# A graph layer on one core: stores of u four slots behind a block's end, reads of u five slots ahead, and the last group's blocks in one line

## The chip, the cores and the metric

The kernel runs on one core of a Trainium2 chip. The metric is the device time of one execution in microseconds, as the median of several runs. A profiled execution gives a page of the busy times and a trace of every instruction. The engines are named TensorE (PE), VectorE (DVE), ScalarE (ACT), GpSimd (POOL) and SyncE (SP, which only issues transfers here).

## The reference

The layer is a relational graph convolution with a highway gate, on 1250 nodes of 1024 features and 20000 edges of 8 types, all in float32:

```python
h = jnp.maximum(_layernorm(x, axis=-1), 0.0)
# with x := h inside the layer
msgs = x[src]
out = x @ root + bias
for r in range(8):
    mask = (edge_type == r).astype(x.dtype)
    sums = jax.ops.segment_sum(msgs * mask[:, None], dst, num_segments=n)
    cnt = jax.ops.segment_sum(mask, dst, num_segments=n)
    out = out + (sums / jnp.maximum(cnt, 1.0)[:, None]) @ weight[r]
u = out
z = jnp.concatenate([u, x], axis=1) @ w_gate + b_gate
result = x_in + jnp.tanh(u) * z + x * (1.0 - z)
```

The kernel uses that a weighted sum of rows can be taken after the product: it computes y = h @ weight[r] for all nodes first, and then adds to each target node the rows of y that its edges name, each times one over the count.

## The kernel before, in words

**Products.** The 1250 nodes are ten blocks of 128 (the last has 98 rows). There are eleven matrices, numbered s: eight relations (s = 0 to 7), root (s = 8), and the two halves of w_gate (s = 9 for h, the last one for u). One call of `step(s, i)` makes the product of two blocks, i and i+5, with matrix s, for i = 0 to 4, so that 50 steps come before the gate. `product` uses Strassen's scheme with seven half-sized products (L283). For s > 0 the first four steps are taken in pairs, and one of the seven is itself split a second time (class `Second`, L210); the pieces are slotted between the others by the table `fill`, whose keys say behind which of the seven they come. For a pair, the first row of the even step is complete only in the odd step: it is held in `waiting`, finished by L237, L238 (for i = 0) or L241 (for i = 2), and then stored by `put` (L380, on SP's queue). For s = 8 and 9, `put` adds a bias on DVE first (L375).

**Row buffers.** Each step takes two row buffers, t[0] and t[1], from a pool of four. ScalarE writes the first product into t[0] (L312), the second into t[1] (L316), the third into t[0] again (L320); DVE adds the others from PSUM (L297, L305). A buffer is free again when its store has landed.

**Edges.** The relations form three groups (0 to 2, 3 to 5, 6 and 7), numbered g. For each group the edges of a node are sorted into slots: the nodes are ordered by their number of edges, and for each block d of the ordered nodes, slot k holds the k-th edge of each. `K[g][d]` is the number of slots of a block: 20, 10, 8, 7, 7, 6, 5, 5, 4, 3 in the first two groups, and 16, 7, 6, 5, 4, 4, 3, 3, 2, 2 in the last. `add_slot` issues one gather on POOL (L1008, rows of y into one of four buffers `got`) and one DVE instruction that adds them, weighted, to the block's sum u (L1016; L1014 for the first of all). The sum of a block starts from what the group before stored: `new_u` takes one of four buffers `u` and reads it back by an indirect DMA on POOL (L463 in a helper). When a block is done, its u is scattered to `u_dram` by an indirect DMA on POOL (L469). In the last group, blocks 4 to 9 go to `last_dram` on SP's queue (`to_last`, L1213) and are read again in the gate; blocks 0 to 3 are held in their buffers and get the row of h @ root added (`add_hr`, L1220).

**Order.** The program is issued in the order written, and each engine keeps its own order. `edges` is a generator that yields once per slot. `spread` advances it evenly between the pieces of the products (seven calls `between(j)` per step), so a gather, an add or a store of the edges stands in the queues of POOL, DVE and SP at a fixed place among the instructions of the products. The first group's edges run beside s = 4 and 5, the second's beside s = 6 and 7, the last's beside s = 8 and 9. In `edges` before, the store of a block and the read of the block after next both come behind slot 1 of the next block; the last group runs two such generators one after the other, blocks 4 to 9 and then 0 to 3 (`held`).

Of the kernel before, what the change touches and what calls it, by code (L numbers as in the profile page):

```python
# [19 lines left out]
def tile_rgcn_highway(  # L20
# [43 lines left out]
    ND = -(-N // P)  # L64
    NP = ND // 2
# [3 lines left out]
    R0 = (0, 3, 6, R)  # L69
# [8 lines left out]
    FAR = 1 << 20  # L78
    CG = 4
    GOT = 4  # L80
    LATE = 4

    A11, A12, A22, S1, S2, S3, S4 = range(7)
# [272 lines left out]
    def paired(s, i):  # L356

        return s > 0 and i < NP // 2 * 2
# [2 lines left out]

    def step(s, i, between=lambda j: None):

        t = [rows.tile([P, D], F32, name="row") for _ in range(2)]
        two = paired(s, i)
        if two and i % 2 == 0:
            waiting[i] = Second(fac[s], i), t[0]

        def put(i, part, t):
            d = i + part * NP  # L370
            n = nrows(d)
            at = slice(d * P, d * P + n)
            if s >= ROOT:
                to = (hr_dram, z_dram)[s - ROOT][at, :]
                nc.vector.tensor_add(t, t, bias_bc)  # L375
            else:
                g = max(k for k in range(G) if R0[k] <= s)
                o = (s - R0[g]) * N + d * P
                to = y[g][o:o + n, :]
            nc.sync.dma_start(to, t[:n])  # L380

        def beside(j):
            new = fac[s + 1]
            if i == 0 and j == 0 and s > 0:
                fac[s].make_t4()
            if two and i == 0:
                sums(j)
            if two and (i, j) == (1, 6):
                Second(fac[s], 2).left()
            if (s, i, j) == (0, 0, 3) or (s > 0 and (i, j) == (3, 0)):  # L390
                new.load_first()
            if (s, i, j) == (0, 0, 3) or (s > 0 and (i, j) == (3, 2)):
                new.load_next()
            if i == NP - 1:
                if j == 0:
                    new.load_b22()
                elif j == 1:
                    new.make_t1()
                elif j == 3:
                    new.load_b21()  # L400
                    new.make_t2()
                elif j == 4:
                    new.make_t3()
            between(j)

        def sums(j):


            e = waiting[0][0]
            for k in range(4) if s > R0[1] and j == 0 else (j,) if s <= R0[1] and j < 4 else ():  # L410
                e.right(k)
            if j == (0 if s > R0[1] else 4):
                e.left()

        fill = {}
        if two:
            e, to = waiting[i - i % 2]
            if i == 0:
                fill = dict(sixth=lambda: (e.second(), e.second_to_first(to)))
            elif i == 1:  # L420
                fill = dict(first=lambda: e.first(),
                            fifth=lambda: (e.sixth(), True),
                            sixth=lambda: (e.seventh(), e.to_first(to), 0)[-1],
                            seventh=lambda: (e.fourth(), e.to_second(t[0]), 0)[-1],
                            third=lambda: (e.fourth_to_second(t[0]), put(i - 1, 0, to), 0)[-1])
            elif i == 2:
                fill = dict(sixth=lambda: e.first(),
                            seventh=lambda: e.sixth(),
                            third=lambda: (e.seventh(), e.to_first(to), 0)[-1],
                            fourth=lambda: (e.fourth(), True))  # L430
            else:
                fill = dict(first=lambda: (e.to_second(t[0]), e.fourth_to_second(t[0]), 0)[-1],
                            sixth=lambda: (e.second(), True),
                            seventh=lambda: (e.second_to_first(to), put(i - 1, 0, to), 0)[-1])
        product(h_op[i], fac[s], t, between=beside, whole=not two, fill=fill)
        for part in range(2):
            if part or not two or i % 2:
                put(i, part, t[part])
# [543 lines left out]

    with ExitStack() as edges_part:
        gpool = edges_part.enter_context(tc.tile_pool(name="gpool", bufs=GOT))
        upool = edges_part.enter_context(tc.tile_pool(name="upool", bufs=4))
        bias_bc = edges_part.enter_context(tc.tile_pool(name="bpool", bufs=1)).tile(
            [P, D], F32, name="bias_bc")
        nc.sync.dma_start(bias_bc, bias[None, :].to_broadcast([P, D]))
# [16 lines left out]
        def add_slot(u, g, d, k, at, w, first=False):  # L1005
            n = nrows(d)
            t = got()
            nc.gpsimd.indirect_dma_start(  # L1008
                out=t[:n], out_offset=None, in_=y[g][:, :],
                in_offset=bass.IndirectOffsetOnAxis(ap=at[:n, d, k:k + 1], axis=0),  # L1010
                bounds_check=y[g].shape[0] - 1, oob_is_err=False)
            w = w[:n, d, k:k + 1]
            if first:
                nc.vector.tensor_scalar(u[:n], t[:n], w, None, op0=OP.mult)  # L1014
            else:
                nc.vector.scalar_tensor_tensor(u[:n], t[:n], w, u[:n], op0=OP.mult, op1=OP.add)  # L1016
# [3 lines left out]
        def new_u(d, of=None, g=0):  # L1020

            n = nrows(d)
            u = upool.tile([P, D], F32, name="u")
            if of is not None:
                rows_of(u[:n], of[:, :], node[:n, g, d:d + 1])
            return u

        def edges(g, blocks, to, late=0):


            of = u_dram[g - 1] if g else None
            ahead = new_u(blocks[0], of, g)
            behind = []
            for _ in range(late):
                yield

            def leave():
                while behind:
                    to(*behind.pop())

            for d in blocks:
                u = ahead
                last = K[g][d] - 1
                for k in range(last + 1):
                    add_slot(u, g, d, k, idx[:, g], w_of[:, g], first=g == 0 and k == 0)
                    if k == min(1, last):
                        leave()
                        if d != blocks[-1]:
                            ahead = new_u(d + 1, of, g)
                    yield  # L1050
                behind.append((d, u))
            leave()
            yield

        def u_back(g):
            def to(d, u):
                n = nrows(d)
                to_rows(u_dram[g][:, :], u[:n], node[:n, g, d:d + 1], f"u{g}")

            return to  # L1060
# [42 lines left out]
        def beside(e, total, s, i, last):  # L1103


            between = spread(e, total, 7 * ((last - s) * NP + NP - i))
            while s <= last:
                step(s, i, between)
                s, i = next(steps, (NM, 0))
            return s, i  # L1110
# [13 lines left out]
        def with_others(e):  # L1124

            others = other_groups()
            for k, _ in enumerate(e):
                yield
                if k % 2:
                    next(others, None)  # L1130
            for _ in others:
                pass

        weights(0)
        s, i = beside(with_others(edges(0, range(ND), u_back(0))), sum(K[0]) + 1, s, i,
                      R0[2] - 1)
        def with_passes(e):
            passes = passes_needed()
# [4 lines left out]
        for g in range(1, G - 1):  # L1143
            e = edges(g, range(ND), u_back(g), LATE)
            e = with_passes(e) if g == G - 2 else e
            next(e)
            s, i = beside(e, sum(K[g]) + LATE, s, i, R0[g + 2] - 1)


        passes = nc.values_load(n_pass[0:1, 0:1], min_val=0, max_val=E // MORE,  # L1150
# [64 lines left out]
        def add_hr(d, u):  # L1215
            n = nrows(d)
            t = got()
            rows_of(t[:n], hr_dram[:, :], node[:n, LG, d:d + 1])
            us[d] = u
            return lambda: nc.vector.tensor_add(u[:n], u[:n], t[:n])  # L1220

        def in_turn(*es):
            for e in es:
                yield from e

        def place_of(what, i, part):

            o = ("z", "d").index(what)
# [55 lines left out]
                while adds:  # L1284
                    adds.pop(0)()

        def held():

            new, old = [], []
            for _ in edges(LG, range(HELD), lambda d, u: new.append(add_hr(d, u))):  # L1290
                yield
                for add in old:
                    add()
                old, new[:] = new[:], []
            for add in old + new:
                add()

        late = edges(LG, range(HELD, ND), to_last, LATE + 1)
        next(late)
        between = spread(in_turn(late, held()), sum(K[LG]) + 2 + LATE, 7 * ((NM - 2 - s) * NP + NP - i))  # L1300
        while s < NM - 1:
            def beside_h(j):
                between(j)
# [69 lines left out]
```

## Time and profile before

| | |
|---|---|
| median of 3 runs | 1382.97 us (1379.1 to 1385.62) |
| profiled execution | 1378.6 us, of which the profile's span is 1376.8 us |
| busy: PE, DVE, POOL, ACT | 1353.1, 928.6, 632.6, 365.3 us |
| L1008, gathers of y on POOL | 202 issues, 252.0 us busy, 6.3 us from issue to landing |
| L1016, adds of edges on DVE | 192, 245.5 us, 1281 ns each |
| L469, stores of u on POOL | 20 issues, 26.4 us |
| u read back from u_dram | 20 issues, 7.3 us from issue to landing |

An engine's busy time counts its own instructions, not the time of the transfers that it issues. A row of the profile names the line, the engine, the operation and what it writes and reads (out<-in), and often, in brackets or behind a bar, the idle time of the engine before it and what ended that. "us to landing" is the time from the issue of a transfer to the semaphore that tells of its end. The granted clock is the share of full speed at which TensorE was allowed to run.

### The profile page before, as it was taken

The page shows a single profiled execution, that of the slowest core. Times are in us where ns is not written, and L with a number is a line of the kernel's source. Part 1 is how long each engine was busy: PE and PEld are TensorE (multiplying, and loading weights), DVE is VectorE, ACT ScalarE, POOL GpSimd, SP SyncE. Part 2 cuts the span into 40 slices and gives each one's busy share as a digit, 9 for nine tenths or more (in the row PEclk, how much of TensorE's full clock was granted, in tenths as well). Part 3 has the DMA queues.
Part 4 walks back from the last instruction along what each step waited for, and adds up shares of the span by engine and source line. Part 5 has one row for each costly group of instructions (what it writes and reads, how often), then busy time and mean ns, then how long its engine had stood idle before and what let it go on. Part 6 is the DMA issues. An engine that isn't in the chain of part 4 may idle for free.

```text
span 1376.8 us, 12702 instructions
## 1 busy us (share of the span) xinstructions
PE 1353.1 (98%) x3786; PEld 656.9 (48%) x3786; DVE 928.6 (67%) x1842; ACT 365.3 (27%) x793; POOL 632.6 (46%) x567
## 2 busy tenths in 40 slices
PE   7999999999999999999999999999999999999997
PEld 4544455445545544544554454455445445544443
DVE  6956977897768826547455854854566674567985
ACT  3335666566621111111111111111111111121220
POOL 0003655665561634667674533455535433335641
PEclk9999999999999999999999999999999999999999
DMA  8764655854653285359879736877959752687861
GB/s 303 286 203 98 130 118 137 204 97 134 138 140 104 65 229 114 118 198 263 227 243 330 246 112 220 309 253 241 338 166 325 271 189 94 216 280 241 286 201 58
DMA packets 110011, 272.78 MB, mean 198 GB/s; under 512 B 25906, under 2 KB 27936, under 8 KB 109808
## 3 DMA queue, kind: packets, MB, share of 16 engines
q0 software_dynamic: 48864, 128.60, 30.0%
q1 hardware_dynamic: 45232, 111.86, 26.4%
q10 hardware_dynamic: 15840, 31.46, 7.1%
q8 instruction: 30, 0.49, 0.1%
q14 instruction: 45, 0.37, 0.1%
HBM read 214.20 MB, written 80.65 MB: 214 GB/s over the span
## 4 chain that ended last, share of the span: by engine, by line
PE 70%; issue 8%; DVE 6%; DMA 6%; POOL 3%; ACT 1%; POOLq 0%; DVEq 0%; ACTq 0%
PE ps L283 62%; PE ps L210 7%; DMA got<-y,idx 4%; POOL got L1008 2%; DMA u_dram<-u,node 1%; DMA w<-in_L_gnn_weight_dram 1%; PE ps_n L755 0%; DVE seen L760 0%; DVE u L1016 0%; DVE junk L820 0%; DMA y<-row 0%; DMA u<-last_dram 0%; DMA got<-h_dram,node 0%; DVE row L1321 0%; DVE h_op L1257 0%
## 5 line engine op out<-in xcount | busy, mean ns | idle before, releaser
L283 PE MATMUL ps<-w,h_op 128*128 128x512 f32 x2800 | 1232.1, 594 | 2.9 <-ACT row L316 2.7
L283 PEld LDWEIGHTS ps<-w,h_op 128*128 128x128 f32 x2800 | 525.9, 191 | 606.5 <-issue 590.9
L1008 POOL DMA_INDIRECT got<-y,idx x202 | 252.0, 1248 | 268.7 <-DVE u L1016 177.5
L1016 DVE SCALAR_TENSOR_TENSOR u<-got,w_of,u 128x1024 f32<-128x1024 f32 (+1 forms) x192 | 245.5, 1281 | 161.7 <-DMA got<-y,idx 152.6
L834 POOL DMA_INDIRECT table<-row_col,at_i x157 | 176.4, 1123 | 150.4 <-DVE at_i L830 71.2
L305 DVE TENSOR_TENSOR row<-row,part 128x512 f32<-128x512 f32 x55 | 37.8, 688 | 94.4 <-ACT part L304 94.4
L338 ACT COPY row<-ps 128x512 f32<-128x512 f32 x50 | 29.3, 585 | 237.0 <-PE ps L283 231.3
L304 ACT COPY part<-ps 128x512 f32<-128x512 f32 x55 | 32.1, 584 | 181.4 <-PE ps L283 181.4
L312 ACT COPY row<-ps 128x512 f32<-128x512 f32 x55 | 32.2, 585 | 168.2 <-PE ps L283 165.3
L297 DVE TENSOR_TENSOR row<-row,ps 128x512 f32<-128x512 f32 x55 | 37.5, 683 | 57.9 <-PE ps L283 48.7
L210 PE MATMUL ps<-w,w 128*128 128x256 f32 x288 | 71.5, 381 | 0.0
L316 ACT COPY row<-ps 128x512 f32<-128x512 f32 x55 | 32.2, 585 | 141.6 <-PE ps L283 124.6
L320 ACT COPY row<-ps 128x512 f32<-128x512 f32 x55 | 32.2, 585 | 139.8 <-PE ps L283 139.6
L210 PEld LDWEIGHTS ps<-w,w 128*128 128x128 f32 x288 | 54.1, 190 | 19.0 <-issue 13.4
L469 POOL DMA_INDIRECT u_dram<-u,node x20 | 26.4, 1318 | 73.2 <-DVE u L1016 67.1
L820 DVE SCALAR_TENSOR_TENSOR junk<-k_bc,key_col,before 128x128 f32<-128x128 int32 x157 | 54.9, 350 | 4.2
L500 POOL DMA_INDIRECT node_dram<-ids,pos_i x30 | 38.6, 1285 | 39.3 <-issue 38.7
L210 PE MATMUL ps<-w,h_op 128*128 128x256 f32 x216 | 56.3, 383 | 0.0
L760 DVE TENSOR_TENSOR seen<-seen,ps_n 128x110 f32<-128x110 f32 x157 | 42.1, 268 | 16.8 <-PE ps_n L755 12.7
L210 PEld LDWEIGHTS ps<-w,h_op 128*128 128x128 f32 x216 | 40.1, 190 | 23.0 <-issue 19.9
L737 ACT ACTIVATE is_lo<-io,less_lo 128x128 bf16<-128x128 f32 x157 | 50.1, 390 | 0.9 <-DVE row L305 0.9
L888 DVE SCALAR_TENSOR_TENSOR junk<-v_bc,val,one 128x1280 bf16<-128x1280 f32 x30 | 46.5, 1550 | 4.1 <-DMA v_bc<-val_dram 3.3
(182 smaller groups left out, 948.6 us busy)
## 6 DMA issues: line engine op xcount, KB each, us to landing
y<-row SPq DMA_DIRECT2D x72, 512.0 KB, 6.5
w<-in_L_gnn_weight_dram ACTq DMA_DIRECT2D x21, 1024.0 KB, 9.4
w<-in_L_gnn_weight_dram SPq DMA_DIRECT2D x11, 1024.0 KB, 9.3
k_bc<-keys_dram SPq DMA_DIRECT2D x39, 256.0 KB, 4.0
l_bc<-los_dram SPq DMA_DIRECT2D x39, 256.0 KB, 5.9
w<-in_L_gnn_w_gate_dram ACTq DMA_DIRECT2D x6, 1024.0 KB
h_dram<-h_op SPq DMA_DIRECT2D x9, 512.0 KB, 6.9
hr_dram<-row SPq DMA_DIRECT2D x9, 512.0 KB, 6.1
```

The costliest lines, as they stand in the source:

```text
L210: nc.tensor.matmul(p, a[:, k, :], b[:, k, :], start=(fresh and k == 0), stop=(k == 1), skip_group_check=True)
L283: nc.tensor.matmul(b[:, at], aop[:, i, k, :], w.of[i][:, k, at], start=(fresh and k == 0), stop=(k == KQ - 1), skip_group_check=True)
L297: nc.vector.tensor_add(c12, c12, c)
L305: nc.vector.tensor_add(c22, c22, d)
L500: ins = nc.gpsimd.indirect_dma_start(out=node_dram[g][:, :], out_offset=bass.IndirectOffsetOnAxis(ap=pos_i[:, g, d:d + 1], axis=0), in_=id ...
L737: nc.scalar.activation(is_lo[:, i, :], io, AF.Abs, bias=less_lo[:, c0 + i:c0 + i + 1])
L760: nc.vector.tensor_add(seen[j][:, i, :], was, p[:, i, :])
L820: nc.vector.scalar_tensor_tensor(junk, o["k_bc"][:, i, :], key_col[:, c:c + 1], before, op0=OP.is_equal, op1=OP.mult, accum_out=rank[:, c: ...
L834: ins = nc.gpsimd.indirect_dma_start(out=table[:, :], out_offset=bass.IndirectOffsetOnAxis(ap=at_i[:n, i:i + 1], axis=0), in_=row_col[:n, ...
L888: nc.vector.scalar_tensor_tensor(junk, v_bc[:, g, :], val[:, c:c + 1], one.to_broadcast([P, KEYS]), op0=OP.is_gt, op1=OP.mult, accum_out=p ...
L1008: nc.gpsimd.indirect_dma_start(out=t[:n], out_offset=None, in_=y[g][:, :], in_offset=bass.IndirectOffsetOnAxis(ap=at[:n, d, k:k + 1], axis=0),
L1016: nc.vector.scalar_tensor_tensor(u[:n], t[:n], w, u[:n], op0=OP.mult, op1=OP.add)
```

## The change

The generator `edges` is written anew around one counter t, the slot. For each block it works out where its slots start (`starts`), when its u leaves (`leaves`: four slots, GOT, after the last slot) and when its u is read (`reads`: five slots before the first, but not before the store that frees its buffer has been issued). What a store returns, the addition of the row of hr, is carried out three slots later. The generator yields six times more after its last slot than before it did, most of which fall to the last call of a group. The last group is one line of blocks, 4 to 9 and then 0 to 3, instead of two generators; `in_turn` and `held` go. Each group's number of calls grows by one.

In `step`, the two row buffers are exchanged for i = 2, and the held row of i = 0 is put one piece earlier (behind the "seventh" instead of the "third").

```diff
+    UB = 4
...
+        two = paired(s, i)
         t = [rows.tile([P, D], F32, name="row") for _ in range(2)]
-        two = paired(s, i)
+        if two and i == 2:
+            t.reverse()
...
-                            seventh=lambda: (e.fourth(), e.to_second(t[0]), 0)[-1],
-                            third=lambda: (e.fourth_to_second(t[0]), put(i - 1, 0, to), 0)[-1])
+                            seventh=lambda: (e.fourth(), e.to_second(t[0]), put(i - 1, 0, to),
+                                             0)[-1],
+                            third=lambda: (e.fourth_to_second(t[0]), 0)[-1])
...
         def edges(g, blocks, to, late=0):
             of = u_dram[g - 1] if g else None
-            ahead = new_u(blocks[0], of, g)
-            behind = []
-            for _ in range(late):
+            nb = len(blocks)
+            starts = [late + sum(K[g][d] for d in blocks[:b]) for b in range(nb + 1)]
+            leaves = [starts[b + 1] - 1 + GOT for b in range(nb)]
+            reads = [max(-1, starts[b] - 5, leaves[b - UB] if b >= UB else -1) for b in range(nb)]
+            u, then = {}, {}
+            for t in range(-1, leaves[-1] + 4):
+                for b, d in enumerate(blocks):
+                    if starts[b] <= t < starts[b + 1]:
+                        k = t - starts[b]
+                        add_slot(u[d], g, d, k, idx[:, g], w_of[:, g], first=g == 0 and k == 0)
+                for b, d in enumerate(blocks):
+                    if t == leaves[b]:
+                        then[t + 3] = to(d, u[d])
+                if then.get(t):
+                    then[t]()
+                for b, d in enumerate(blocks):
+                    if t == reads[b]:
+                        u[d] = new_u(d, of, g)
                 yield
-            def leave():
-                while behind:
-                    to(*behind.pop())
-            for d in blocks:
-                u = ahead
-                last = K[g][d] - 1
-                for k in range(last + 1):
-                    add_slot(u, g, d, k, idx[:, g], w_of[:, g], first=g == 0 and k == 0)
-                    if k == min(1, last):
-                        leave()
-                        if d != blocks[-1]:
-                            ahead = new_u(d + 1, of, g)
-                    yield
-                behind.append((d, u))
-            leave()
-            yield
...
-        late = edges(LG, range(HELD, ND), to_last, LATE + 1)
-        next(late)
-        between = spread(in_turn(late, held()), sum(K[LG]) + 2 + LATE, 7 * ((NM - 2 - s) * NP + NP - i))
+        blocks = [*range(HELD, ND), *range(HELD)]
+        last = edges(LG, blocks, lambda d, u: (add_hr if d < HELD else to_last)(d, u), LATE)
+        next(last)
+        between = spread(last, sum(K[LG]) + 2 + LATE, 7 * ((NM - 2 - s) * NP + NP - i))
```

More of the change, by code (lines that the diff above doesn't have):

```diff
@@ L984, in tile_rgcn_highway @@
         gpool = edges_part.enter_context(tc.tile_pool(name="gpool", bufs=GOT))
-        upool = edges_part.enter_context(tc.tile_pool(name="upool", bufs=4))
+        upool = edges_part.enter_context(tc.tile_pool(name="upool", bufs=UB))
         bias_bc = edges_part.enter_context(tc.tile_pool(name="bpool", bufs=1)).tile(
@@ L1134, in tile_rgcn_highway @@
         weights(0)
-        s, i = beside(with_others(edges(0, range(ND), u_back(0))), sum(K[0]) + 1, s, i,
+        s, i = beside(with_others(edges(0, range(ND), u_back(0))), sum(K[0]) + 2, s, i,
                       R0[2] - 1)
@@ L1146, in tile_rgcn_highway @@
             next(e)
-            s, i = beside(e, sum(K[g]) + LATE, s, i, R0[g + 2] - 1)
+            s, i = beside(e, sum(K[g]) + LATE + 1, s, i, R0[g + 2] - 1)
         passes = nc.values_load(n_pass[0:1, 0:1], min_val=0, max_val=E // MORE,
@@ L1220, in add_hr @@
             return lambda: nc.vector.tensor_add(u[:n], u[:n], t[:n])
-        def in_turn(*es):
-            for e in es:
-                yield from e
         def place_of(what, i, part):
@@ L1285, in gate_load @@
                     adds.pop(0)()
[L1287 to L1296, printed above, removed]
-        late = edges(LG, range(HELD, ND), to_last, LATE + 1)
-        next(late)
-        between = spread(in_turn(late, held()), sum(K[LG]) + 2 + LATE, 7 * ((NM - 2 - s) * NP + NP - i))
+        blocks = [*range(HELD, ND), *range(HELD)]
+        last = edges(LG, blocks, lambda d, u: (add_hr if d < HELD else to_last)(d, u), LATE)
+        next(last)
+        between = spread(last, sum(K[LG]) + 2 + LATE, 7 * ((NM - 2 - s) * NP + NP - i))
         while s < NM - 1:
```

## The prediction

> **What bounds the kernel now.** I read the engines' busy shares first, then TensorE's gaps, then what stood behind the only gap in the part that is changed. From the page (busy us, share, instructions; then a group's busy time, mean ns and idle time before it):
>
> ```profile
> PE 1353.1 (98%) x3786; PEld 656.9 (48%) x3786; DVE 928.6 (67%) x1842; ACT 365.3 (27%) x793; POOL 632.6 (46%) x567
> L283 PE MATMUL ps<-w,h_op 128*128 128x512 f32 x2800 | 1232.1, 594 | 2.9 <-ACT row L316 2.7
> ```
>
> TensorE is busy 98% of the span. A busy matmul row can hide poor packing, so I looked at spacing: in the timeline eight 512-wide records take 3.43 us and 56 of them 24.28 us, 0.43 us each, in every stage. From 390 us to the last matmul at 1369.7 us there is one gap in TensorE's timeline (its row gives start, length, and in brackets the idle time before it and its releaser):
>
> ```profile
> 750.00 25.97 PE L283 MATMUL ps<-w,h_op 128*128 128x512 f32 x56 [2.74 <-ACT row L316]
> ...
> 1206.35 24.28 PE L283 MATMUL ps<-w,h_op 128*128 128x512 f32 x56
> ```
>
> The same 56 matmuls take 25.97 us after the gap and 24.28 us elsewhere. Busy time by window (the 0.83 is the granted clock) says why:
>
> ```profile
> core 0: us, PE busy (x), PEclk, DMA share, GB/s
> 745.00:755.00 10.00, 7.26 (x14) 0.83 0.94 362
> 755.00:765.00 10.00, 10.00 (x24) 1.00 0.63 207
> ```
>
> (1 - 0.83) x 10 us = 1.7 us are lost to a slower clock right after the gap, which agrees with 25.97 - 24.28 = 1.69. The gap therefore costs 2.74 + 1.7 = 4.4 us. Between 76 and 390 us, the sorting stage, gaps of 0.2 to 1.5 us add up to 5.0 us, none released by a store; the clock stays at 1.00 there.
>
> What stood behind the gap is read from the four engines' timelines around it (ACT, SP, DVE twice, POOL twice):
>
> ```profile
> 749.37 0.59 ACT L316 COPY row<-ps 128x512 f32<-128x512 f32 x1 [8.30 <-DMA y<-row]
> ...
> 743.72 1.81 SPq L380 DMA_DIRECT2D y<-row  x3
> ...
> 740.28 1.28 DVE L1016 SCALAR_TENSOR_TENSOR u<-got,w_of,u 128x1024 f32<-128x1024 f32 x1 [5.54 <-DMA got<-y,idx]
> ...
> 743.28 0.41 DVE L241 TENSOR_TENSOR row<-row,ps 128x256 f32<-128x256 f32 x1
> ...
> 731.55 1.28 POOL L469 DMA_INDIRECT u_dram<-u,node  x1 [3.85 <-DVE u L1016]
> 733.14 1.01 POOL L1008 DMA_INDIRECT got<-y,idx  x1 [0.30 <-issue]
> ```
>
> Backwards in time: POOL stood 3.85 us at a store of u, because DVE had not finished that block. The gathers behind it went out at 733.14 and later. DVE waited 5.54 us for one. L241, which completes the row held back since product i=2, stood behind it in DVE's order and came at 743.28. SP stored the row at 743.72, it landed 5.55 us later, and only then could ACT write the recycled row buffer. So a slack of one product was used up by one POOL wait. Over the whole run (us, times, longest):
>
> ```profile
> POOL got L1008 <- DVE u L1016: 177.5, 61, 14.2
> DVE u L1016 <- DMA got<-y,idx: 152.6, 60, 7.1
> POOL u_dram L469 <- DVE u L1016: 67.1, 17, 7.6
> ```
>
> The first is harmless: POOL waits for a free gather buffer, four slots ahead of DVE. The third is what takes that lead away; the second is its result.
>
> **What the skill says.** The Trainium skill, "Perfetto Trace Analysis", Identifying the Most-Contended Engine, says that matmul busy time is a poor measure; the trace agrees (mean record 594 ns, spacing 430). "TensorE: Matmul & The Clock Gate", Part 1, says that an idle window of about 3.4 us halves TensorE's clock and a busy one of that length restores it. Here 2.74 us of idle was enough, 1.47 us was not, and the loss of 1.7 us is half of 3.4. "DMA: Bandwidth & Descriptors", Anatomy of one DMA, says that the issuing engine, not the DMA engine, waits for semaphores; POOL's 3.85 us in front of a gather that was ready shows it.
>
> **The change, part by part.** No instruction is added or removed in the compute: the 20 stores of u (L469, 1.3 us of POOL each), 6 stores to last_dram, 20 reads and 192 adds stay, so engine sums move by nothing.
>
> *Stores four slots behind.* A store issued at slot L+4 follows a gather into the buffer that slot L has just released, so it finds its u finished. At block ends inside a group POOL's waits go; I put the 67.1 us at 15 to 25, since the last store of each of two groups still waits. POOL's share of the wait moves into the harmless row. The DVE wait of 152.6 us should fall to about 100: what remains is gathers that take 6.3 us (page). Price on TensorE: the gap of 4.4 us goes if L241 comes 2.8 us earlier; the saved POOL wait alone is 3.85.
>
> *Reads of u five slots ahead.* Before, a read came K-1 slots ahead, one slot in the last group's blocks of two. A slot is 238 us/79 = 3.0 us in the second group and 238/58 = 4.1 in the last; five slots are 15 to 20 us against 7.3 us to landing. In the second group the buffer has long been stored. In the last, blocks d=9 and d=0 are read at the very slot whose store frees their buffer, and POOL must wait for that SP store: about 6 us each, 12 in all, with gathers queued behind. Gathers are 16 us ahead there, so I price this at 0 on TensorE; without that cover, see the second rival.
>
> *One line of blocks.* The read of d=0 was issued directly ahead of its first add; it is now ahead by four to five slots. The row of hr is added three slots after its gather (12 us against 6.2). DVE's 7.3 us at that junction is hidden behind dense TensorE: 0.
>
> *One slot more per group, six calls after the last.* The spacing shrinks by 1/80; the leftover calls hold two stores at 1.3 us of POOL, with the next group's first add some 15 us off: 0.
>
> *The swap of rows for i=2, and the earlier store of i=0's held row.* The first copy L312 at 740.47 ran before the store at 743.72 was issued, the second waited: buffers are handed out in the order in which they were freed, the later one to t[1]. After the swap at i=2 the later one is t[0], so L312 needs it one product, 3.4 us, sooner than L316 did. Moving put ahead of S4 gives time back only where DVE or SP worked behind it. In s=8 and 9 the bias add (1.22 us) now follows L245: at 1047.6 and 1165.2 us instead of 1050.8 and 1169.6, for copies at 1054.3 and 1173.0, so a 5.6 us landing is in time. In s=2 the put passes two key loads. In s=3 to 7 it gives nothing, because SP waited for DVE itself:
>
> ```profile
> SPq L380 <- DVE row L238: 87.5, 5, 23.5
> ```
>
> In s=5 L238 ended at 691.50 and L312 of i=2 ran at 693.15; the store would hold it to 697.1, 4.0 us. TensorE has 2.8 us in hand there (the 3.43 us of S1 less the 0.59 us copy), so 1.2 us would be lost if DVE stays as late as now. With DVE earlier, 0; bounds 0 and 3 us for all nine s.
>
> **Sum.** The profiled execution took 1378.6 us (span 1376.8). Less 2.74 and 1.7: 1374.2. The median of the runs shown is 4.4 us above that execution; its cause isn't traced. It is the size of one more such gap, and I take it that most of it is, because DVE comes near its limit elsewhere too: L316 waited for a row store three times, 15.8 us in all, and only once did it reach TensorE. I forecast **1375.5**, leaving 1.3 us for the swap and for gaps that stay.
>
> **Rivals.** *The gap stays or moves* (0.31): four gather buffers and a 6.3 us landing may keep DVE late whatever POOL's order, and the store of i=2's row is still completed by L241. For it: 61 buffer waits. Against it: a cycle of gather, landing and add is about 9 us for four slots, 2.3 a slot against 3.0 available. Time: 1379 to 1383.
>
> *A new wait in the last group* (0.10): SP's store that frees d=0's buffer stands behind the store of an hr row, which waits for DVE (the one of product i=2 left at 1078.1). It lands near 1085, POOL's next gather near 1093, and DVE is 6 us late at 1087. The row of i=2, issued at 1095.4 now, would go near 1098.5, landing near 1104.5 for a copy at 1105.0, which has another 2.8 us. A landing of 10 us turns that into a gap of 3 us plus 1.7: about 1379.
>
> *Slower* (0.09): the swap's tighter L312, if the new order makes DVE later. The spare time of each step by the trace is 9.0 us in s=4, -1.2 in s=5, 13.6 in s=6, 6.2 in s=7, 3.9 in s=8, 5.1 in s=9. DVE late by another 7 us costs 8.2 + 0.8 + 3.1 + 1.9 = 14.0, plus up to four clock losses of 1.7: about 1393 with the old gap gone. Below some 6.5 us it is not slower. Against it: nothing in the change gives DVE work.
>
> **Numbers.** Half a per cent (6.9 us) is about what a measurement can tell here, and it begins at 1376.05, next to the forecast. The forecast case (0.50; its own range is 1373 to 1377.5) I split 0.44 faster and 0.06 same; the first rival gives 0.28 same and 0.03 faster; the second 0.09 same and 0.01 slower; the last 0.08 slower and 0.01 same. Together faster 0.47, same 0.44, slower 0.09. The range 1371.5 to 1385 reaches from the sum, with half of the sorting stage's 5.0 us of gaps thrown in, to the first rival's end.
>
> **What would show it.** Right: no gap over 0.5 us after 390 us and no window with a clock under 0.95 there until the end; POOL's wait at L469 under 25 us; DVE's wait for gathers near 100; L316's wait for y<-row near 0. Wrong: L312 waiting for y<-row with TensorE idle behind it (the swap), a POOL read of u waiting 6 us followed by a late L241 near 1095 (the second rival), or a gap that stays with POOL's waits gone (the first).

## The result and the profile after

The changed kernel takes 1374.8 us (median of 7 runs, 1372.84 to 1374.99) against 1382.97 (median of 7, 1379.1 to 1385.62): a ratio of 0.9942, with a 95% interval of 0.9927 to 0.9958. It is faster by 0.6%, and its runs spread over 2.2 us instead of 6.5. The profiled execution took 1372.9 us, its span is 1371.1.

Lines that the text names have new numbers in the changed kernel's file: L283 is now L284, L297 L298, L316 L317, L320 L321, L380 L383, L241 L242, L463 L467, L469 L473, L1008 L1012, L1016 L1020, L1213 L1216 and L1220 L1223. The page, and the busy time by window around the place of the old gap (busy us, granted clock, DMA share, GB/s):

```profile
PE 1350.0 (98%) x3786; PEld 655.2 (48%) x3786; DVE 931.4 (68%) x1842; ACT 365.2 (27%) x793; POOL 632.0 (46%) x567
...
L284 PE MATMUL ps<-w,h_op 128*128 128x512 f32 x2800 | 1229.2, 593 | 1.3 <-DVE row L298 0.8
```

```profile
740.00:750.00 10.00, 10.00 (x25) 1.00 0.91 318
750.00:760.00 10.00, 10.00 (x25) 1.00 0.52 196
```

TensorE's idle time ahead of L284 is 1.3 us instead of 2.9, only 0.2 of it released by an ACT copy, and the clock is 1.00 where it was 0.83. From 500 to 1230 us the whole window is busy, 730.0 of 730 us; before it was 727.3. The chain at that place, in the four engines' timelines (ACT, SP, DVE, POOL twice):

```profile
741.53 0.58 ACT L317 COPY row<-ps 128x512 f32<-128x512 f32 x1 [2.80 <-PE ps L284]
...
733.55 2.04 SPq L383 DMA_DIRECT2D y<-row  x3
...
733.11 0.41 DVE L242 TENSOR_TENSOR row<-row,ps 128x256 f32<-128x256 f32 x1
...
723.94 1.03 POOL L473 DMA_INDIRECT u_dram<-u,node  x1 [0.19 <-issue]
...
737.15 1.61 POOL L473 DMA_INDIRECT u_dram<-u,node  x1 [0.19 <-issue]
```

POOL goes straight through both stores of u shown. DVE completes the row at 733.5, SP stores it at once, and it has 8.0 us to land before ACT needs the buffer. ACT then waits for the matmul alone. The waits over the run:

```profile
POOL got L1012 <- DVE u L1020: 197.1, 84, 14.2
...
DVE u L1020 <- DMA got<-y,idx: 124.8, 60, 10.8
...
POOL u L467 <- DMA last_dram<-u: 33.4, 3, 15.4
...
POOL u_dram L473 <- DVE u L1020: 11.7, 1, 11.7
POOL u_dram L473 <- DVE far_k L1083: 10.8, 1, 10.8
```

At the stores of u 22.5 us are left; before it was 67.1 us for the adds and 5.7 us for another DVE instruction (L1080, now L1083). Both waits that are left stand at a group's last block. DVE waits 28 us less for gathers. The third line is new.

The span is 5.7 us shorter, of which the gap is 4.4. At 290 us TensorE was already 2.3 us ahead, but that is not the change's: in three profiles of the kernel before, its last wait of the start-up ended at 76.3, 76.6 and 73.8 us, here at 73.6. And 1.3 us were lost again in the gate, where new gaps of 0.65 and 0.16 us in TensorE show.

### The profile page after: what moved, and what is told of

Same layout as the page of the kernel before. It is cut to its first block, busy times and chain, and to the rows that moved or that the text cites. A ratio compares the mean times of both kernels' runs of the same rounds, so it can differ in the third digit from the quotient of the medians.

```text
span 1371.1 us, 12725 instructions
## 1 busy us (share of the span) xinstructions
PE 1350.0 (98%) x3786; PEld 655.2 (48%) x3786; DVE 931.4 (68%) x1842; ACT 365.2 (27%) x793; POOL 632.0 (46%) x567
## 4 chain that ended last, share of the span: by engine, by line
PE 78%; DVE 6%; issue 6%; DMA 3%; POOL 1%; ACT 1%; POOLq 0%; DVEq 0%; ACTq 0%
PE ps L284 70%; PE ps L211 8%; DMA w<-in_L_gnn_weight_dram 1%; POOL got L467 1%; DVE junk L824 1%; DMA got<-hr_dram,node 0%; DMA h_op<-z_dram,node 0%; DVE seen L764 0%; PE ps_n L759 0%; POOL out_dram L473 0%; DMA got<-y,idx 0%; DVE row L1310 0%; DVE h_op L1256 0%; DVE u L1223 0%; DVE w L170 0%
## 5 line engine op out<-in xcount | busy, mean ns | idle before, releaser
L284 PE MATMUL ps<-w,h_op 128*128 128x512 f32 x2800 | 1229.2, 593 | 1.3 <-DVE row L298 0.8
L284 PEld LDWEIGHTS ps<-w,h_op 128*128 128x128 f32 x2800 | 524.3, 190 | 603.4 <-issue 587.3
L1012 POOL DMA_INDIRECT got<-y,idx x202 | 257.2, 1273 | 280.3 <-DVE u L1020 197.1
L1020 DVE SCALAR_TENSOR_TENSOR u<-got,w_of,u 128x1024 f32<-128x1024 f32 (+1 forms) x192 | 246.2, 1284 | 127.4 <-DMA got<-y,idx 124.8
L298 DVE TENSOR_TENSOR row<-row,ps 128x512 f32<-128x512 f32 x55 | 37.6, 684 | 66.2 <-PE ps L284 57.6
L321 ACT COPY row<-ps 128x512 f32<-128x512 f32 x55 | 32.1, 584 | 143.8 <-PE ps L284 143.8
L317 ACT COPY row<-ps 128x512 f32<-128x512 f32 x55 | 32.1, 584 | 134.6 <-PE ps L284 128.0
L467 POOL DMA_INDIRECT u<-u_dram,node x20 | 23.0, 1148 | 51.7 <-DMA last_dram<-u 33.4
```

The costliest lines, as they stand in the source:

```text
L284: nc.tensor.matmul(b[:, at], aop[:, i, k, :], w.of[i][:, k, at], start=(fresh and k == 0), stop=(k == KQ - 1), skip_group_check=True)
L298: nc.vector.tensor_add(c12, c12, c)
L1012: nc.gpsimd.indirect_dma_start(out=t[:n], out_offset=None, in_=y[g][:, :], in_offset=bass.IndirectOffsetOnAxis(ap=at[:n, d, k:k + 1], axis=0),
```

## The experiments

Twelve kernels ran, in four groups; the kernels of one group shared a chip and the runs of the kernel before. The absolute times differ between groups (before: 1391.1, 1385.6, 1379.5 and 1378.9 us), so ratios are compared. One number is worked out from each trace, the **row's lateness**: the time from the start of the third copy (L320) of step i = 3 to the end of L241, which completes the row held since i = 2. In the first profile of before it is 12.9, 17.9, 12.2 and 14.9 us in s = 4 to 7; in the changed kernel 8.7, 10.1, 8.6 and 8.0.

**Part by part (first group).**

The rows alone:

```diff
 # on the kernel before
+        if two and i == 2:
+            t.reverse()
+ seventh=lambda: (..., put(i - 1, 0, to), 0)[-1]
- third=lambda: (..., put(i - 1, 0, to), 0)[-1]
```

> The kernel before with the row part of the change alone: exchanged row buffers at i = 2, and the held row of i = 0 put one piece earlier. Theory (POOL's waits at the stores of u make DVE late, and that is what the change removes): DVE's lateness stays, so the time stays within 0.2% of before, 1380 to 1385 us; L316 of i = 4 still waits for y<-row, a TensorE gap of 1 to 4 us may be there; POOL's wait at L469 stays at 60 to 70 us. L312 of i = 2 in s = 5 may wait as well (up to 4 us), which could add up to 3 us. Rival (the rows are what frees the path): 1373 to 1377 us, no gap after 390 us.

Measured: 0.9986 of before (0.9959 to 1.0013). POOL's wait at the stores is 71.4 us, the lateness 11.0, 19.1, 12.0 and 17.0, and TensorE has two gaps behind the same copy, 4.05 us in s = 5 and 3.07 in s = 7. The rows give nothing that can be measured.

The new generator alone:

```diff
 # on the changed kernel
-        if two and i == 2:
-            t.reverse()
- seventh=lambda: (..., put(i - 1, 0, to), 0)[-1]
+ third=lambda: (..., put(i - 1, 0, to), 0)[-1]
```

> The kernel after with the row part undone: the new generator of edges alone. Theory: all of the gain is here, 1373 to 1376.5 us, no TensorE gap of over 0.7 us after 390 us, POOL's wait at the stores of u under 30 us. In s = 8 and 9 the put of i = 0 comes 4 us later again, which is covered because L316 of i = 2 needs it, not L312. Rival (the rows): 1380 to 1385 us, a gap at L316.

Measured: 0.9937 (0.9912 to 0.9962), the whole gain; lateness 9.1, 8.5, 8.5 and 9.2, no gap over 0.6 us from 302 us on. The absolute times of this group, here 1380.6 us, all lie above what was expected, as this chip was slower with every kernel, before included.

The reads of u back:

```diff
-reads = [max(-1, starts[b] - 5, leaves[b - UB] if b >= UB else -1) for b in range(nb)]
+reads = [-1] + [max(starts[b - 1] + 1, leaves[b - UB] if b >= UB else -1) for b in range(1, nb)]
```

> The kernel after with the reads of u back where they were, behind slot 1 of the block before; stores four slots behind as in the change. Theory: the stores carry the gain; 1373 to 1376.5 us, DVE up to 7 us late for a read in the last group's short blocks, with no TensorE gap over 1 us from it, POOL's wait at the stores under 30 us. Rival (the earlier reads carry it): 1380 us or more, with DVE waiting for u.

Measured: 0.9936 (0.992 to 0.9952). The earlier reads carry nothing here: late ones cost no time.

The stores back (a read that waits for a store to be issued moves with it):

```diff
-leaves = [starts[b + 1] - 1 + GOT for b in range(nb)]
+leaves = [starts[b + 1] - 1 + 2 for b in range(nb)]
```

> The kernel after with the stores of u back at two slots behind a block's last slot, where the kernel before had them; reads stay five slots ahead, the last group stays one line, and the rows stay as in the change. Theory: POOL waits for DVE at the stores again (50 us or more in all), the adds of edges are late, the row held for i = 2 lands late in s = 4 to 7; 1378 to 1384 us with a TensorE gap of 1 to 4 us at the second copy of i = 4. Rival (reads or rows carry the gain): 1373 to 1376 us, and no gap.

Measured: 0.9976 (0.9957 to 0.9995), so most of the gain is gone, with the reads, the single line and the rows all in place. The waits of this kernel, and its one gap after 390 us:

```profile
DVE u L1020 <- DMA got<-y,idx: 153.1, 59, 8.1
...
POOL u_dram L473 <- DVE u L1020: 61.3, 17, 7.1
...
ACT row L317 <- DMA y<-row: 32.7, 6, 13.2
```

```profile
764.07 26.62 PE L284 MATMUL ps<-w,h_op 128*128 128x512 f32 x56 [7.63 <-ACT row L317]
```

POOL's 61 us and DVE's 153 are close to those of the kernel before, 67 and 153. The lateness in s = 5 is 21.6 us. Of the parts that were taken back one at a time, only the place of the stores costs the gain. The single line was not taken back by itself, and the stores were not moved without it, so that they are enough on their own is not shown.

**Dose and repeat (second group).** Three slots instead of four:

```diff
-leaves = [starts[b + 1] - 1 + GOT for b in range(nb)]
+leaves = [starts[b + 1] - 1 + 3 for b in range(nb)]
```

> The changed kernel with the stores of u three slots behind instead of four. Theory (a store waits exactly when POOL reaches it before DVE has done the block's last slot; each slot of lead is one slot of waiting): POOL's waits at the stores between those of two slots (61 us) and of four (23 us), some 35 to 45 us; the row of i = 2 is completed earlier than with two, and the time is nearer to the whole change than to before: 0.994 to 0.997 of before. Rival (any store position that differs from the old one does as well, since what matters is traffic at that moment and not POOL's wait): POOL's wait need not lie between, and the time is that of four slots.

Measured: 0.9948 (0.993 to 0.9966), beside 0.9949 (0.9931 to 0.9967) for the changed kernel itself in this group. POOL's waits at the stores for DVE's adds are 22.9 us, against 11.2 for four slots here and 61.3 for two in the first group; with those for other DVE instructions they are 37.6, 21.4 and 77.7. The lateness is 9.1, 9.9, 8.3 and 7.8. The waits lie between either way; the 35 to 45 expected fits the second sum and not the first. The time is that of four slots, so this run does not tell the two theories apart by time: with three slots the row is already early enough.

The changed kernel and the generator alone, once more:

> The changed kernel itself, beside the variants below on one chip. All theories: 0.993 to 0.995 of before; no gap of over 1 us in TensorE from 400 us to the gate.

> The new generator without the row part, now on one chip with the whole change. Theory (the rows give nothing once DVE is early): within 0.2% of the whole change. Rival (the rows give a part): slower than the whole change by 2 us or more, with L316 of i = 2 or i = 4 waiting for a row store while TensorE stands still.

Measured: 0.9949 (0.9931 to 0.9967) and 0.994 (0.9921 to 0.9958), 1378.9 and 1377.0 us. The rows give nothing on top of the generator.

**What a gap costs.** A ladder of delays on ScalarE, behind the first copy of i = 4:

```diff
+    ladder = {4: 9, 5: 12, 6: 15, 7: 18, 8: 21, 9: 24}
...
+            if i == NP - 1 and j == 0 and s in ladder:
+                for _ in range(ladder[s]):
+                    nc.scalar.copy(t_small[0], t_small[0])
             between(j)
```

> The changed kernel with 9, 12, 15, 18, 21 and 24 extra copies of a small tile on ScalarE ahead of the second copy of i = 4 in s = 4 to 9, some 0.33 us each, so that this copy is late by 3 to 8 us and TensorE stands still for this less 2.85 us: gaps of about 0, 1, 2, 3, 4 and 5 us. They measure what a gap of a given length costs. Theory: gaps of about 1.5 us and less cost their own length; those of about 2 us and more cost another 1.7 us each through 3.4 us at half clock, so the span is 15 us of gaps and about 7 us of clock longer than that of the changed kernel. Rival (the half clock at 750 us was a coincidence of one execution): no loss of clock behind these gaps, and 15 us longer.

Measured: three gaps instead of five, because ScalarE has more slack than I had allowed: the extra copies took 6.99, 8.15 and 9.32 us in s = 7 to 9, and each gap is 5.8 us shorter (in the changed kernel's timeline ScalarE is idle 2.80 us before the second copy and 2.85 us before the third). In TensorE's timeline, and in the windows around them:

```profile
989.87 24.30 PE L284 MATMUL ps<-w,h_op 128*128 128x512 f32 x56 [1.23 <-ACT row L317]
...
1111.24 26.00 PE L284 MATMUL ps<-w,h_op 128*128 128x512 f32 x56 [2.35 <-ACT row L317]
...
1235.48 6.47 PE L284 MATMUL ps<-w,h_op 128*128 128x512 f32 x8 [3.52 <-ACT row L317]
```

```profile
985.00:995.00 10.00, 8.77 (x21) 1.00 0.95 325
1110.00:1120.00 10.00, 8.76 (x17) 0.83 0.93 363
1234.00:1244.00 10.00, 8.52 (x26) 0.66 0.29 114
```

After 1.23 us of idle the 56 matmuls take their 24.3 us. After 2.35 us they take 26.0, and the clock of that window is 0.83: 1.7 us more, as in the first profile. After 3.52 us the clock is 0.66, a loss of 3.4 us in the window, 0.6 of it inside the gap. So the slow clock was no coincidence, and it belongs to gaps of about two microseconds and more. The three gaps and the 1.7 and 2.8 us of clock lost outside them make 11.6 us; the single run took 1390.6 us, 11.7 more than the changed kernel in this group. The 15 and 7 us expected were for five gaps.

**Another link of the same chain (third group).** The kernel before, with the stores of u left alone and the row completed and stored one piece earlier:

```diff
-                            sixth=lambda: (e.second(), True),
-                            seventh=lambda: (e.second_to_first(to), put(i - 1, 0, to), 0)[-1])
+                            sixth=lambda: (e.second(), e.second_to_first(to),
+                                           put(i - 1, 0, to), True))
```

> The kernel before, edges and their stores untouched, with the row held for i = 2 completed (L241) and put one piece earlier in i = 3, right behind its last matmuls instead of behind the seventh product. It cuts the suspected chain at another link: POOL still waits at the stores of u and DVE is still late, but the row store stands at least one add of edges ahead, 3 to 5 us. Theory (the late row store is the only way in which DVE's lateness reaches TensorE): POOL's wait at the stores stays at 60 to 75 us, the gaps at the second copy of i = 4 in s = 4 to 7 go or shrink to under 1 us, and 0.993 to 0.997 of before. Rival (POOL's waits cost time by other ways too): 0.998 to 1.001 of before, with gaps elsewhere.

Measured: 0.9953 (0.9937 to 0.997). Its waits and its windows:

```profile
DVE u L1016 <- DMA got<-y,idx: 140.6, 68, 7.2
...
POOL u_dram L469 <- DVE u L1016: 61.8, 16, 8.4
```

```profile
500.00:1250.00 750.00, 750.00 (x1931) 1.00 0.67 226
```

POOL waits 61.8 us, nearly as before, DVE waits 140.6 us for its gathers instead of 152.6, and TensorE has no gap at all from 500 to 1250 us: the lateness is 9.0, 7.5, 7.1 and 3.8. POOL's waits cost nothing by themselves that these runs can tell; they reach TensorE through this one row and its buffer.

The kernel before, two more profiles:

> The kernel before once more, for a second profile of it. Theory (the gap behind L316 is one of several that come and go between executions): one to three gaps of 2 to 5 us at the second copy of i = 4 in s = 4 to 7, each of over 2 us followed by 3.4 us at half clock; the span is longer than that of the changed kernel by about the sum of these. Rival (the gap of the first profile was alone of its kind): the same single gap in s = 5, or none.

> The kernel before once more, for a third profile. Theory and rival as for the second profile; in particular the sum of gaps and clock losses differs between profiles by several us, and the spans with it.

In TensorE's timeline, of the first and of the second:

```profile
749.95 26.00 PE L283 MATMUL ps<-w,h_op 128*128 128x512 f32 x56 [2.33 <-ACT row L316]
...
991.79 26.00 PE L283 MATMUL ps<-w,h_op 128*128 128x512 f32 x56 [2.14 <-ACT row L316]
```

```profile
983.97 24.30 PE L283 MATMUL ps<-w,h_op 128*128 128x512 f32 x56 [1.65 <-ACT row L316]
```

The first has gaps in s = 5 and s = 7, each with its slow 56 matmuls: 2.33 + 2.14 + 2 x 1.7 = 7.9 us. The second has one of 1.65 us in s = 7, and no loss of clock. With the 4.4 us of the original profile this makes 7.9, 4.4 and 1.65 us for spans of 1380.8, 1376.8 and 1371.3 us. The gaps change from execution to execution, and the spans go with them (the start-up, which differs by 2.8 us, is the other part).

Over all thirteen profiles without the ladder the lateness tells where a gap is: the seven values of 15.2 us and more all come with a gap at the second copy of i = 4 in their s, and none of the 45 of 14.9 us and less does.

The sorting stage, where the generator does not run yet, adds to the scatter. Near 275 us four of the fourteen profiles have a gap of 3.25 to 4.90 us (three with the new generator, one with the old), the others none over 2.11.

**Both links (fourth group).** The third group's diff on the changed kernel:

> The changed kernel with the row held for i = 2 completed and put one piece earlier as well, so that both links of the chain are relieved. Theory (either relief alone already closes the gaps, and TensorE is then without a gap from 400 us to the gate): no further gain, 0.993 to 0.996 of before, as with each of them alone; the row of i = 2 in s = 8 no longer lands late. Rival (lateness left over still costs time): 0.992 or less.

Measured: 0.9956 (0.994 to 0.9973). The lateness is down to 3.8, 1.3, 1.3 and 1.3 us, no copy waits for an hr row any more, and nothing more is gained. No version beats the changed kernel by an amount that these runs can tell.

## Why the prediction was right

**The bound and the price.** The forecast was 1375.5 us by taking away one gap of 2.74 us and its 1.7 us of slow clock; measured 1374.8. Gap and clock loss are gone, and the ladder shows both prices separately. That the numbers meet so closely is in part luck: the 1.3 us left for the swap and for gaps that stay were lost in the gate, for a reason that the forecast did not have.

**The chain.** A store of u, POOL's lead, a late gather, a late row, a late buffer: read link by link in the timelines, and broken at two of the links. Putting the stores back brings it back (0.9976); moving the row instead breaks it further down (0.9953).

**The step from the profiled execution to the median.** The 4.4 us by which the runs lay above that execution I took to be mostly further gaps of this kind. The two added profiles of before support it, with 7.9 and 1.65 us in place of 4.4, and so does the spread: 6.5 us before, 2.2 us after. For every run, profiled or not, the record has the mean granted clock: in the third group 0.9972 over the eleven of before and 0.9987 over the six with the row early, in the fourth 0.9973 and 0.9990 (seven of the version with both links). That is 2.1 and 2.4 us of lost clock more, or one to one and a half losses of 1.7 us a run. In which stage they fall isn't recorded.

**POOL's waits at the stores** were put at 15 to 25 us; they are 22.5, in the places named, 11.7 of it in the row of the waits that was 67.1.

**DVE's wait for gathers** was put at about 100 us; it is 124.8. In the first two groups of edges it fell from 142.6 to 93.8 us. In the last group it rose from 10.0 to 31.0 us, and the term below is behind it.

**The reads in the last group** were the mis-sized term: two reads that wait about 6 us each, 12 in all. There were three, and 33.4 us (the second view shows how the chain ends, on ACT):

```profile
1043.97 0.95 POOL L467 DMA_INDIRECT u<-u_dram,node  x1 [12.36 <-DMA last_dram<-u]
...
1055.22 0.96 POOL L467 DMA_INDIRECT u<-u_dram,node  x1 [5.60 <-DMA last_dram<-u]
...
1075.56 0.95 POOL L467 DMA_INDIRECT u<-u_dram,node  x1 [15.44 <-DMA last_dram<-u]
```

```profile
1098.56 0.59 ACT L317 COPY row<-ps 128x512 f32<-128x512 f32 x1 [3.38 <-DMA hr_dram<-row]
```

This is the second rival, and it did happen: the store that frees the buffer stood on SP behind an hr row, left at 1071.45, and POOL waited 15.44 us for it. I had counted the landing, but not the time in which POOL already stood at the read before SP could issue the store. The row of i = 2 in s = 8 then landed about half a microsecond after ACT wanted it (3.38 us idle instead of 2.85), well inside the 2.8 us that TensorE has in hand. So the price on TensorE was 0 as forecast, with less cover than it seemed. With the late reads POOL waits for the same stores 11.5 us instead of 33.4 and the time is the same: in the last group the five slots made POOL wait longer and bought nothing that these runs can tell.

**The rows** were priced at 0 with bounds of 0 and 3 us; two comparisons (the rows alone against before, and the generator alone against the whole change) show nothing either way. The slower rival, which rested on them, needed DVE 7 us later, and DVE came earlier.

**Not foreseen** is a loss in the gate. With it the first sign of being right, no gap over 0.5 us after 390 us, is not met to the letter: one of 0.65 us stands at 1255 us. A gap of 0.4 to 1.3 us behind L298 stands there in eight of the nine profiles with the new generator (not in that with the stores at two slots) and in none of the five with the old one. In the changed kernel L298 stands in DVE's order behind two additions of hr rows that wait 7.85 us for their gathers. The kernel before waits 7.57 us at the same place without a gap, and its L297 ends 5.3 us after the product that TensorE has begun there, where L298 ends after 4.2 us here. So lateness alone does not explain it, and the cause is open.

## What to carry to other kernels

When the bound engine's one gap is released by a copy, follow it through the queues until an engine waits that nobody seems to need: here a store of 1.3 us, put into a gather queue one slot too soon, became a gap in TensorE five links later. Put a store in an in-order queue behind the point at which its data is sure to be ready, as many slots as that queue runs ahead (four here, and three did as well); or give the transfer at the end of the chain more room, which did as well here within what these runs can tell, and is a smaller edit. And price a gap in TensorE with the slow clock that follows it.

## What the runs showed of the hardware

TensorE's clock fell to one half for stretches of 3.4 us around idle times of about 2 us and more. After the start-up, gaps of 1.80 us and less were followed by full clock in these traces, and gaps of 2.14 us and more by one to three such stretches (two around those of 3.52 and 4.71 us, three around 7.63); of two gaps between, in the sorting stage of two variants, the one of 2.01 us was followed by half clock and the one of 2.11 us was not. That is shorter than the 3.4 us idle window in the Trainium skill, "TensorE: Matmul & The Clock Gate", Part 1; here the measurement decides. A 7.63 us gap added only 2.3 us to the 56 matmuls behind it (26.62 against 24.28), as more than half of its slow clock passed while TensorE was idle anyway.

What settles it in these traces is not the gap's length but how much of it falls into one stretch. In each trace the clock changes only at whole multiples of 3.413 us from its first rise to full clock. Cut there, the windows read (us, busy us of TensorE, granted clock, DMA share, GB/s) for the gap of 2.74 us in the kernel before, for the one of 2.01 us (`after_reads_late`) and for the one of 2.11 us (`edges_only_again`):

```profile
746.57:749.98 3.41, 0.69 (x2) 1.00 1.03 420
749.98:753.39 3.41, 3.39 (x4) 0.50 0.93 358
```

```profile
270.11:273.53 3.42, 1.41 (x8) 1.00 0.90 231
273.53:276.94 3.41, 3.41 (x6) 0.50 0.48 102
```

```profile
273.78:277.19 3.41, 3.19 (x8) 1.00 0.58 84
277.19:280.61 3.42, 1.54 (x7) 1.00 0.84 22
280.61:284.02 3.41, 3.11 (x12) 1.00 0.28 54
```

The gap of 2.01 us lies in one stretch and halves the clock of the next. The gap of 2.11 us is divided into 0.22 and 1.88, and the clock stays. In all fourteen traces a stretch at full clock with 2.01 us of idle time or more was followed by one at half clock, and one with 1.96 us or less never was. So a gap a little over 2 us long can cost its own length in one execution and 1.7 us more in another.
